# A four-layer convolution, attention and expert kernel: room, order of the last projection, depth of weight prefetch, and norm steps at the borders of its layers

## The chip, the cores and the metric

The kernel runs on one core of a Trainium2 chip. TensorE (PE) does the matrix products, VectorE (DVE) and ScalarE (ACT) the elementwise work, GpSimd (POOL) small things and some transfers, and SyncE (SP) issues most transfers. The metric is the device time of one execution in microseconds; the kernel before has a median of 3357.86 us over three runs (3353.48 to 3364.4). One further execution was recorded by the hardware profiler; all lines shown come from it. A code such as L506 is a line of the kernel before.

## The reference, cut to what matters

The input `x` is 8 x 384 x 32 x 32 in float32. Four layers follow, each `x = x + layer(gn(x))`, where `gn` normalizes each image over 32 groups of channels.

```python
# layer 0: convolutional attention, 8 heads of 48 channels
q, k, v = (einsum(pw_i, gelu(bn(depthwise3x3(x, dw_i)))) for i in "qkv")
out = bn(einsum(w_out, softmax(q.T @ k * scale) @ v))
# layer 1: 4 experts, the two best of each position mixed
out = sum_e coef_e * (w2_e @ relu(w1_e @ x + b1_e) + b2_e)
# layer 2: depthwise 7x7, reflecting edges
out = depthwise7x7(x, w) + b
# layer 3: channels in four chunks; chunks 0, 2 through a small MLP with gelu,
# chunks 1, 3 through depthwise k x k; three branches k = 1, 3, 5
x1, x2, x3 = branch(x, 1), branch(x, 3), branch(x, 5)
w = softmax(fusion(mean(x1 + x2 + x3)))
out = (x1 * w0 + x2 * w1 + x3 * w2) @ proj_w + proj_b
```

The batch norms `bn` of layer 0 run over all images and positions, so the projections can only begin when a whole convolution, of all eight images, is done. The group norms need one image each, but the kernel computes the coefficients of all images together.

## The kernel before, in words

**Tiling.** Channels lie in three blocks `ct` of 128 partitions, an image is 1024 positions. All products are float32; the profile counts each such product as two rows.

**Layer 0's convolutions** are products with banded weights (L373). Their results leave PSUM through ACT into one of two large buffers tagged `o` (L414). `results` then transposes each image on DVE (L342), takes its statistics (L164) and stores it to memory as `raw[v][b]` from SP (L344). The order of convolutions is such that v's last block comes last. The pool `co` that holds the `o` buffers closes before attention opens its pools, so attention's tiles lie in the room of it, and of the other tiles that closed with it.

**Attention** (`attention`, L437). `fetch` loads the inputs of one image; `activate(b, v)` applies the batch norm and gelu of input v on ACT, in three pieces; `project` (L506) makes k and q in 18 products each (36 rows); `spread` puts each of three tiles of the result into kT or qT, where the tile's pieces for other partitions are copied by ACT (k of the first image, L524) or DVE (L526, L528). The scale vector `own`, a mask, is made on POOL (L464 to L473). `project_v` (L553) makes v and DVE copies it into vT (L557), which POOL has set to one beforehand (L475). `scores` (L600) and the exponential on ACT (L607), then `attend` (L619) and `project_out` (L675) run over eight images, two halves, the pairs of heads and groups of positions. The very last half image has its own code at L750 to L767: `attend`, then nine products with `w_last`, then the norm of the last tile on DVE (L635 to L640), then three products which need that norm; the result z is copied by ACT (L765) and stored by POOL (L766). Three pools of PSUM tiles of two banks each, tag `sc`, rotate under k, q, v, scores and the outputs.

**Layer 1** runs the experts over images (L875, L1088). SP loads its first weights `w1` (L783), and its tiles, during attention.

**Layer 2** convolves with 7x7 banded weights (L1429): for each `ct`, eight steps `c`, each of two halves `e` of 56 rows. `load_weights` (L1152) issues the next weight tile on ACT's queue (L1159) into one of two `lw` buffers, and POOL adds the reflected edge (L1163); `next_weights` (L1168) spreads a landed tile into a `wx` buffer on ACT (L1176), and calls `load_weights` when it has spread the last part of a tile. `evict` (L1370) takes PSUM out by ACT into `o`. `finish` (L1276) then, image by image: DVE transposes `o` into `y`, adds bias and the residual `r2` (loaded by SP, two buffers), SP stores `y` to `y2mem`, DVE takes statistics, POOL copies edges (L1301). `finish_all(ct)` is stepped while the next block's convolution runs. `prepare` loads layer 2's own third input.

**Layer 3.** Its norm is done in steps: `gn_steps` (L171) first averages the means over the groups (PE, L191; DVE, L202 to L205), yields, then averages the variances (PE), takes the inverse root (DVE L158, POOL L159) and makes s and t (L209). `norm01` covers the first two channel blocks, `norm3` all. `prepare3(unit, q)` loads an input into an `xn2` buffer (two of them), applies s and t on ACT (L224) and transposes into the padded convolution input on DVE (L1348). Unit 1 holds the middle chunk (pairs of half images, `pair_s`, `pair_t`, L1457), unit 0 the first block. `convolve3(1, 5)` and `convolve3(1, 3)` (L1396) run with unit 1, step by step, while `finish_all(2)` ends; after the norm, `hidden3` (L1582 to L1607) makes the MLP's hidden values, with inputs loaded by POOL (L1587) and a bias from t (L1500). After it come unit 0's convolutions, a reordering on POOL, the fusion weights (L1740 to L1761) and the last projections (L1807 to L1818).

**What sets the order.** On PE, ACT and DVE the instructions stay in the order in which the code writes them (`manual_schedule`, L259); in layer 0's convolutions and in layers 2 and 3 this holds for POOL too. Elsewhere, for SP everywhere and for POOL in attention, a planner orders them by the program and by the room they need. Each engine takes its instructions in that order: one that waits holds all behind it. Transfers also use a small set of completion semaphores in turn, so a transfer may be held until an earlier, unrelated transfer with the same semaphore has ended.

## Time and profile before

| | us |
|---|---|
| median of three runs | 3357.86 (3353.48 to 3364.4) |
| the profiled execution's own time | 3360.26 |
| its span | 3358.5 |
| PE busy | 3150.9 (94%) |
| DVE, ACT, POOL busy | 1599.0, 1340.9, 238.1 |

The stages of that execution, in us, with PE's and ACT's busy time in each:

| stage | from - to | length | PE | ACT |
|---|---|---|---|---|
| entry and layer 0's norm | 0 - 50.6 | 50.6 | 12.18 | 16.95 |
| layer 0's convolutions | 50.6 - 287 | 236.4 | 205.57 | 179.42 |
| border to attention | 287 - 372 | 85.0 | 73.24 | 35.15 |
| attention | 372 - 1730 | 1358.0 | 1347.57 | 623.69 |
| attention's end | 1730 - 1756 | 26.0 | 18.09 | 3.52 |
| layer 1 | 1756 - 2848 | 1092.0 | 1061.87 | 248.52 |
| layer 2 | 2848 - 3017 | 169.0 | 154.64 | 95.17 |
| layer 3, to hidden3 | 3017 - 3102 | 85.0 | 46.10 | 58.04 |
| hidden3 and unit 0 | 3102 - 3232 | 130.0 | 110.82 | 69.62 |
| last projections | 3232 - 3358.5 | 126.5 | 120.83 | 10.77 |

In a line of the timeline, the first two numbers are start and duration; then engine, line, operation, output and inputs with their sizes, the number of instructions drawn together, and in brackets how long the engine was idle before and which instruction's end released it. A share of busy time is an average over stages; what an edit is worth is read from the stage that it stands in.

### The profile page before, as it was taken

The numbers are of one execution on the slowest core, as the hardware profiler recorded it, in microseconds if no ns is written. First come the engines' busy times: TensorE is split into PE (matmuls) and PEld (weight loads), VectorE is DVE, ScalarE is ACT, GpSimd is POOL, SyncE is SP. The second block draws the span as 40 slices with busy tenths as digits, with TensorE's granted clock in tenths as the row PEclk, the third lists the DMA queues.
The fourth block names the chain that finished last, engine by engine and source line by source line (L and its number), as shares of the span: only waits on it lengthen the run. The fifth ranks groups of instructions, "written<-read, shape, count | busy, mean of one in ns | idle before, by whom it ended". The sixth has DMA issues, their size and how long they took to land.

```text
span 3358.5 us, 40148 instructions
## 1 busy us (share of the span) xinstructions
PE 3150.9 (94%) x16790; PEld 1473.7 (44%) x16790; DVE 1599.0 (48%) x2189; ACT 1340.9 (40%) x1385; POOL 238.1 (7%) x395
## 2 busy tenths in 40 slices
PE   5897999999999999999989999999999998986989
PEld 4774333343434343433333444444444444655534
DVE  6996344444444444444452554343343332356064
ACT  4875453535354444445334302221121111556520
POOL 3331000000000000000000000000000000121400
PEclk9998999999999999999999999999999998997989
DMA  5886011020101110110017223121121111666666
GB/s 213 287 280 248 32 40 59 24 75 22 69 31 59 40 59 22 57 43 29 22 51 269 92 54 91 49 81 49 47 80 42 44 39 42 241 211 231 219 201 203
DMA packets 97911, 339.65 MB, mean 101 GB/s; under 512 B 14409, under 2 KB 17057, under 8 KB 93369
## 3 DMA queue, kind: packets, MB, share of 16 engines
q1 hardware_dynamic: 73816, 267.73, 23.6%
q10 hardware_dynamic: 13776, 36.90, 3.5%
q0 software_dynamic: 10128, 32.36, 2.9%
q8 instruction: 134, 2.20, 0.3%
q14 instruction: 57, 0.46, 0.0%
HBM read 237.96 MB, written 102.32 MB: 101 GB/s over the span
## 4 chain that ended last, share of the span: by engine, by line
PE 67%; issue 12%; DVE 9%; DMA 7%; ACT 4%; POOL 1%; SPq 0%; ACTq 0%; another core or an unknown queue 0%; POOLq 0%; DVEq 0%
PE av L619 13%; PE sc L600 12%; PE ph L875 9%; PE y L1088 9%; PE sc L506 7%; PE sc L553 4%; PE sc L675 3%; PE ps L1429 2%; DVE stats L164 2%; DVE y L342 2%; DMA w<-in_w 1%; PE po L1810 1%; PE po L1807 1%; PE po L1818 1%; DVE xt L309 1%
## 5 line engine op out<-in xcount | busy, mean ns | idle before, releaser
L607 ACT ACTIVATE e<-sc 128x1024 f32<-128x1024 f32 x512 | 483.1, 1030 | 545.8 <-PE sc L600 545.5
L1088 PE MATMUL y<-hs,w 128*128 128x512 f32 x1152 | 521.5, 594 | 6.2 <-DVE hs L1073 6.2
L875 PE MATMUL ph<-xn,w 128*128 128x512 f32 x1152 | 525.0, 594 | 1.3 <-ACT xn L224 1.3
L600 PE MATMUL sc<-qT,kT 64*128 64x512 f32 x2048 | 477.6, 603 | 10.4 <-ACT e L607 10.4
L619 PE MATMUL av<-e,vT 128*64 128x512 f32 x2048 | 467.5, 598 | 0.0
L879 ACT ACTIVATE hs<-ph,b 128x512 f32<-128x512 f32 x192 | 131.6, 685 | 638.5 <-PE ph L875 632.5
L1088 PEld LDWEIGHTS y<-hs,w 128*128 128x128 f32 x1152 | 217.1, 190 | 282.5 <-issue 258.4
L875 PEld LDWEIGHTS ph<-xn,w 128*128 128x128 f32 x1152 | 216.3, 190 | 268.3 <-issue 259.2
L600 PEld LDWEIGHTS sc<-qT,kT 64*128 64x128 f32 x2048 | 185.6, 186 | 297.5 <-issue 228.7
L1073 DVE TENSOR_TENSOR hs<-hs,cb 128x512 f32<-128x512 f32 x192 | 130.0, 687 | 376.6 <-ACT hs L879 370.6
L619 PEld LDWEIGHTS av<-e,vT 128*64 128x64 f32 x2048 | 135.6, 136 | 316.3 <-issue 316.3
L506 PE MATMUL sc<-y,pw 128*128 128x512 f32 x576 | 254.9, 604 | 14.1 <-ACT kT L524 9.1
L373 PE MATMUL ps<-xt,wx 64*64 64x256 f32 x3456 | 202.1, 392 | 43.1 <-ACT o L414 21.8
L637 DVE RECIPROCAL inv<-sm 128x512 f32<-128x512 f32 x64 | 214.6, 3353 | 2.2
L635 DVE LOAD_MASK_SELECT sm<-av x64 | 0.9, 14 | 420.3 <-PE av L619 420.3
L373 PEld LDWEIGHTS ps<-xt,wx 64*64 64x64 f32 x3456 | 161.3, 139 | 82.8 <-issue 50.6
L506 PEld LDWEIGHTS sc<-y,pw 128*128 128x128 f32 x576 | 110.6, 193 | 157.9 <-issue 139.5
L1429 PE MATMUL ps<-xt,wx 64*64 64x256 f32 x2688 | 158.2, 393 | 19.0 <-ACT wx L1176 13.6
L1078 DVE SCALAR_TENSOR_TENSOR r<-cb,b,r 128x512 f32<-128x512 f32 x192 | 134.3, 745 | 69.0 <-DMA cb<-cfmem 67.7
L414 ACT COPY o<-ps 128x2048 f32<-128x2048 f32 x36 | 135.3, 3763 | 47.0 <-PE ps L373 25.0
L1176 ACT ACTIVATE wx<-w,parity 128x448 f32<-128x448 f32 (+2 forms) x192 | 108.3, 616 | 104.4 <-PE ps L1429 32.8
L1429 PEld LDWEIGHTS ps<-xt,wx 64*64 64x64 f32 x2688 | 106.0, 138 | 70.1 <-ACT wx L1176 17.2
(307 smaller groups left out, 2895.6 us busy)
## 6 DMA issues: line engine op xcount, KB each, us to landing
raw<-y SPq DMA_DIRECT2D x72, 512.0 KB
y<-raw SPq DMA_DIRECT2D x24, 1536.0 KB
xr<-in_x SPq DMA_DIRECT2D x42, 512.0 KB
cb<-cfmem SPq DMA_DIRECT2D x64, 256.0 KB
w<-in_w ACTq DMA_DIRECT2D x36, 384.0 KB
xn<-in_x SPq DMA_DIRECT2D x24, 512.0 KB
x<-in_x SPq DMA_DIRECT2D x16, 768.0 KB
z<-z POOLq DMA_DIRECT2D x16, 768.0 KB, 4.2
```

The source lines that it names most:

```text
L373: nc.tensor.matmul(ps[64 * d : 64 * d + 64, 2 * i + e, cc], lhsT=w[r, 12 * cc + 6 * e + 3 * d + k, :], rhs=xt0s[ct][r, 16 * d + 8 * e + 2 ...
L414: nc.scalar.copy(o.rearrange("p b h (i c) -> p i c (b h)", i=4)[:, :, 2 * u : 2 * u + 2], ps.rearrange("p i c b h -> p i c (b h)"),)
L506: nc.tensor.matmul(ps[:, h, :], lhsT=w[:, ct, pair, :], rhs=y[:, ct, h * HF : (h + 1) * HF], start=ct == 0, stop=ct == NC - 1,)
L553: nc.tensor.matmul(ps[:, m, :C], lhsT=y[:, ct, (m0 + m) * P : (m0 + m + 1) * P], rhs=pw_v[:, ct, :], start=ct == 0, stop=ct == NC - 1,)
L600: nc.tensor.matmul(sc[:, s, :], lhsT=kTs[b][r, pair, m * P : (m + 1) * P], rhs=qTs[b][r, pair, h * HF : (h + 1) * HF], start=True, stop=True,)
L607: nc.scalar.activation(e, sc, AF.Exp, scale=1.0 if shifted else HD**-0.5)
L619: nc.tensor.matmul(av[64 * s : 64 * s + 64, :], lhsT=vT[:, m, c0 : c0 + 64], rhs=e[:, s, :], start=m == 0, stop=m == N // P - 1,)
L637: nc.vector.reciprocal(inv, sm)
L875: nc.tensor.matmul(ph, lhsT=w1[:, e, ct, dc * P : (dc + 1) * P], rhs=xn[:, ct, :], start=ct == 0, stop=ct == NC - 1,)
L1078: nc.vector.scalar_tensor_tensor(out=out[oc], in0=cb[e], scalar=b2[:, oc, e : e + 1], in1=out[oc], op0=ALU.mult, op1=ALU.add,)
L1088: nc.tensor.matmul(py[oc], lhsT=w2[:, e, dc, oc * P : (oc + 1) * P], rhs=hs, start=k == 0, stop=k == len(TODO) - 1,)
L1429: nc.tensor.matmul(ps[64 * d : 64 * d + 64, 2 * i + e, c % 2], lhsT=w[r, d * K7 + k, :], rhs=xts[ct][r, 16 * d + 8 * e + c, :, k : k + H], ...
```

## The change

It has these parts.

1. *Layer 0's start.* Block 1 of the input x is loaded into the second `o` buffer rather than into eight small buffers of a pool of its own; the pool `cy` is opened earlier. With that, the rooms of the pools move.
2. *Attention's start.* Through the moved rooms, kT and qT no longer lie where layer 0's last `o` buffer lay. vT is taken from the pool `ay` when v is first projected, and set to one there. `activate(0, 2)`, v's gelu, stands between the last product of q and its copies, rather than after them.
3. *Attention's end.* Of the nine products with `w_last`, four (two outputs, two tiles) are written ahead of the last `attend`; the first two outputs share one PSUM tile of two banks.
4. *Layer 2's weights.* Up to four tiles are loaded ahead rather than two. Tiles go in turn to two `lw` and two `xn2` buffers; two more are issued by SP at the start.
5. *Layer 3's entry.* `fetch3` issues the eight half loads of unit 1's inputs at block 2, step 5, into four `y` buffers, and `room3` clears the padding there. The second part of `norm01` is written after the first half of step 6. `prepare` of layer 2's third input is spread over six steps instead of four.
6. *norm3 and hidden3.* The first part of `norm3` comes after one step of `convolve3(1, 3)` instead of four, with `prepare3(0, 5)` to `(0, 7)` after or between its parts; the inputs of hidden3 for images 0 and 1 are issued by POOL before its second part; five steps follow instead of two.

```diff
-        x0 = co.tile([P, B, H, 32], FP, tag="o", name="o").rearrange("p b h c -> p b (h c)")
+        x0, x1 = (
+            co.tile([P, B, H, 32], FP, tag="o", name="o").rearrange("p b h c -> p b (h c)")
+            for _ in range(2)
+        )
...
-                x = cx.tile([P, N], FP, tag="x", name="x")
                 nc.sync.dma_start(out=x0[:, b], in_=a["x"][b, :, 0])
-                nc.sync.dma_start(out=x, in_=a["x"][b, :, 1])
+                nc.sync.dma_start(out=x1[:, b], in_=a["x"][b, :, 1])
...
-            vT = aw.tile([P, N // P, HEADS * 64], FP, name="vT")
-            nc.gpsimd.memset(vT, 1.0)
...
                     ps = project(w, t, y)
+                    if between and t == NC - 1:
+                        between()
...
+                if not vTs:
+                    vTs.append(ay.tile([P, N // P, HEADS * 64], FP, tag="vT", name="vT", bufs=1))
+                    nc.gpsimd.memset(vTs[0], 1.0)
...
-                    project_q(b)
-                    if begun:
-                        activate(b, 2)
+                    project_q(b, (lambda: activate(0, 2)) if begun else None)
...
+            outs = two_banks()
+            outs = [outs[:, 0, :], outs[:, 1, :]]
+            project_tiles((NC, 0), range(2))
             av_last = attend(*last, keep=True)
...
+            outs.append(two_banks()[:, 0, :])
+            project_tiles((NC, 0), (2,))
+            project_tiles((1,), range(NC))
...
-        w = lw.tile([P, 4 * K7, W + len(EDGE)], FP, tag="w", name="w")
+        n_loaded.append(c)
+        if k == K7 and more_w and (len(n_loaded) - 2) % 4 > 1:
+            w = more_w[0]()
+        else:
+            w = lw.tile([P, 4 * K7, W + len(EDGE)], FP, tag="w", name="w")
...
-            load_weights()
+            n_placed.append(key)
+
+            if len(n_loaded) - len(n_placed) < (4 if todo_load and todo_load[0][0] == K7 and more_w else 2):
+                load_weights()
...
+    more_w.append(new_xn2)
+    for _ in range(2):
+        load_weights(nc.sync)
...
+    def fetch3(q):
+
+        y = new_y()
+        for half in range(2):
+            nc.sync.dma_start(
+                out=y[64 * half : 64 * half + 64, :], in_=y2mem[HB * half + q][1, 0:64, :]
+            )
+        return y
...
+    def hidden_input(b):
+        ys = [new_y() for _ in range(2)]
+        for j in range(2):
+            nc.gpsimd.dma_start(out=ys[j], in_=y2mem[b][1 + j])
+        return ys
...
                     next_weights()
+                    if (ct, c, e) == (2, 6, 0):
+                        s01, t01 = next(norm01)
...
-                if ct == 1 and c >= 1 and c < 5:
-                    for b in (2 * c - 2, 2 * c - 1):
+                if ct == 1 and c >= 1 and c < 7:
+                    for b in ((0,), (1,), (2,), (3, 4), (5, 6), (7,))[c - 1]:
                         prepare(b)
...
                 if ct == 2 and c == 5:
+                    ys3 = [fetch3(q) for q in range(HB)]
+                    room3(1)
...
-                        prepare3(1, q)
+                        prepare3(1, q, ys3[q])
...
-        for q in range(5, B):
-            next(steps)
-            prepare3(0, q)
         next(steps)
         norm3 = gn_steps((mv3[:, 0], mv3[:, 1]), banks, order="B")
         next(norm3)
+        prepare3(0, 5)
         next(steps)
+        prepare3(0, 6)
         next(steps)
+        hidden_in = {b: hidden_input(b) for b in range(2)}
         s, t = next(norm3)
...
-        next(steps)
-        next(steps)
+        prepare3(0, 7)
+        for _ in range(5):
+            next(steps)
...
-                ys = []
-                for j in range(2):
-                    ys.append(new_y())
-                    nc.gpsimd.dma_start(out=ys[j], in_=y2mem[b][1 + j])
+                ys = hidden_in.pop(b, None) or hidden_input(b)
```

## The prediction

> **What bounds the kernel now.** I read the busy shares first, then the chain that ended last, the waits, and the timeline of each stage that the diff touches.
>
> ```profile
> PE 3150.9 (94%) x16790; PEld 1473.7 (44%) x16790; DVE 1599.0 (48%) x2189; ACT 1340.9 (40%) x1385; POOL 238.1 (7%) x395
> ...
> PE 67%; issue 12%; DVE 9%; DMA 7%; ACT 4%; POOL 1%; SPq 0%; ACTq 0%; another core or an unknown queue 0%; POOLq 0%; DVEq 0%
> ```
>
> TensorE is the bound nearly everywhere, so an edit is worth the TensorE idle time that it removes, no more. The diff removes no matmul. Its room is the holes at three borders.
>
> Layer 0 to attention, timeline of 284 to 358 us (start, duration, operation, idle before and its releaser):
>
> ```profile
> 311.50 1.02 ACT L224 ACTIVATE kT<-sc 128x1024 f32<-128x1024 f32 x1 [18.65 <-DVE y L342]
> ...
> 287.12 18.41 PE L506 MATMUL sc<-y,pw 128*128 128x512 f32 x36 [5.04 <-ACT y L224]
> 314.62 18.32 PE L506 MATMUL sc<-y,pw 128*128 128x512 f32 x36 [9.08 <-ACT kT L524]
> ...
> 336.40 16.98 PE L553 MATMUL sc<-pw_v,y 128*128 128x384 f32 x46 [0.22 <-ACT y L224]
> ...
> 313.99 0.76 SPq L490 DMA_DIRECT2D y<-raw  x1
> ...
> 315.84 0.35 SPq L239 DMA_DIRECT2D w<-in_w  x1
> ```
>
> ACT may not write kT until DVE has transposed layer 0's last outputs, whose room kT takes; so q's projection starts 9.08 us late. The v input is loaded at 313.99, ahead of the experts' weights (the w load of 2304 KB).
>
> Attention's end, then layers 2 and 3:
>
> ```profile
> 1730.39 7.09 PE L619 MATMUL av<-e,vT 128*64 128x512 f32 x32
> 1737.40 10.57 PE L675 MATMUL sc<-att,w_last 128*128 128x512 f32 x24
> ...
> 2985.19 11.10 PE L1429 MATMUL ps<-xt,wx 64*64 64x256 f32 x168 [4.75 <-ACT wx L1176]
> ...
> 3009.62 1.06 PE L191 MATMUL ps<-gn_d,gmatB 128*128 128x8 f32 x8 [1.80 <-ACT o L1370]
> ...
> 3029.52 8.74 PE L1396 MATMUL ps<-x,wx 64*64 64x128 f32 x240 [12.54 <-DVE x L1348]
> ...
> 3086.23 5.40 PE L1396 MATMUL ps<-x,wx 64*64 64x128 f32 x96 [6.83 <-DVE gn_m L202]
> ...
> 3098.44 0.62 PE L1500 MATMUL ps<-t,mw 128*72 128x8 f32 x4 [2.32 <-DVE t L1495]
> 3101.65 8.80 PE L1595 MATMUL ps<-y,mw1s 128*72 128x512 f32 x16 [2.59 <-DMA y<-y]
> ```
>
> TensorE is dense at attention's end. Layer 3 holds 12.54 + 6.83 + 2.32 + 2.59 = 24.28 us of idle.
>
> **What the Trainium skill says.** "DMA: Bandwidth & Descriptors", section "Queues, rings and completion order": each DMA engine consumes a queue's descriptors in the order of its ring. So a large SP transfer issued first delays the next one; no line of this trace shows such a pair alone. Its section "Anatomy of one DMA" gives about 2.0 us beside the data's time; in the trace hidden3's first input (512 KB), issued at 3097.70, frees TensorE at 3101.65, 3.95 later, of which the data take some 1.2, so a little more than stated. "TensorE: Matmul & The Clock Gate", section "What's actually happening": after about 3.4 us idle the array runs at half clock until about 3.4 us of work have passed. The trace agrees: 36 projection rows take 18.3 to 18.4 us after idles of 5.04 and 9.08, and 36 x 10.57 / 24 = 15.9 at the dense rate.
>
> **The parts.**
>
> *Start of layer 0* (x1 in the second `o` buffer): 0. The weights still wait for the small bn_gb load, and DVE's eight transposes (36.24 to 50.32) still set TensorE's start at 50.58. The second buffer is first needed at the first eviction, 57.55, after those. Without that cover the first eviction would wait some us.
>
> *Border to attention.* kT, qT in other room removes the 18.65 of ACT. k's projection ends at 287.12 + 18.41 = 305.5. kT's ACT work of one tile (three or four pieces of 1.0) keeps pace with 12 rows x 0.44 = 5.3, so q runs 305.5 to 321.4, against 332.9. If v followed at once, scores would move by 15 to 16. It does not, by my reading. In the changed program SP's order is: pw_v and w_out early, the raw stores, then w1, then the v input. w1's room still hangs on DVE's bn_t, so it is issued at 315.84 as now, and the v input behind it at about 316.3 instead of 313.99. DMA moved 411 to 482 GB/s from 314.5 to 329.8, here 0.42 MB/us for estimate. 2.36 MB of w1 and 1.57 MB of v input take 9.4 us; with some 1.5 us of latency v lands near 327.3. ACT's three gelus (3.5) end near 331, and q's last eviction, now behind them on ACT, near 332; DVE copies it by 335, before v's third group needs that bank. Before, the gelus ended at 337.48 and v's matmuls at 353.38, so 15.9 later; now 331 + 15.9 = 346.9, plus about 1.5 for a cold restart after 8 us idle, 348.4. Gain 5.0. Ends: the v input does not wait behind w1, 16; it lands 3 us later still, 2. vT's memset on POOL (3.51) now waits for the last raw stores, issued by 311.7, and ends near 321: hidden under the v load. `own` moves ahead of bn_s on POOL and is done long before q.
>
> *Steady attention*: 0; dense TensorE covers it.
>
> *Last projection split.* The same 24 rows (10.57) in another order. Now 18 of them (7.9) lie between the last av row at 1737.4 and the six that need its norm, which DVE ends at 1742.4 (0.72 + 3.35 + 0.69 and the gaps, 5.0). After, 8 of the 24 go ahead of the last 16 av rows: av ends near 1737.4 + 8 x 0.44 = 1740.9, its norm near 1745.9, and the 10 rows that remain as cover at 1745.3, so 0.6 of wait. outs[0] and outs[1] now share a tile, so the second product of the six waits for ACT's copy of the first (0.58) and the way there and back, some 0.9. Cost +1.5; ends +0.3 and +3. The z store behind it gates layer 1, so all of it is on the path.
>
> *Layer 2's weights four ahead.* Two buffers xn2 join lw. POOL's edge add then meets landed weights: the waits `ACT wx <- POOL w` (18.1 us, longest 5.4, most of it hidden) go. But the 4.75 at 2985.19 comes from ACT's own queue: ACT idles 8.93 there until an r2 load is in, as its weight DMA is issued in turn on a completion semaphore shared with SP. That stays. From 2848 to 3010 TensorE idles about 16 us, of which 2 to 5 are fresh weights. What is saved ahead of 2940 is partly held by DVE's finish chain with its two r2 buffers. Gain 1; ends: gain 5, loss 2 (two more 532 KB loads beside load3's).
>
> *Layer 3's entry.* The eight half loads of y2 go out near 3000, into `y` buffers, so no pair waits for xn2 (before: last load 3026). The norm's second half moves ahead by one half-step (3.2). But its matmul still needs ACT's eviction; and ACT's first layer-3 weight DMA now waits, in turn, for the second fetched half (SP issues it after the y2 store that follows DVE's last 2998.6, so it lands near 3003). Queued behind it on ACT: a spread (1.2) and the eviction (3.7), ending 3008.4. So the norm matmul comes at 3008.4 against 3009.62, and TensorE waits 3.8 there instead of 1.8; the three half-steps that remain (9.6) end at 3019 against 3017. gn_s 2.91, pair copies 2.1: 3014.8. A spread waiting for TensorE is ahead of the four affines: first affine ends 3018.1, four transposes of 1.85 end 3025.5. Gain 4.0; ends: gain 9 (the fetch is early), loss 1. POOL's memset of x goes ahead of gn_s: 0.59, done in its idle.
>
> *Norm3 and hidden3's input.* The first norm3 matmul follows one step of the 3x3 convolution, not four, and needs DVE's last bn_aggr (ends 3075.46 in DVE's timeline) and an eviction (3073.8 in ACT's). These move with the entry by 4 to 5: 3070.7. TensorE waits there, but weights then lie ready for two steps (2 x 1.45). From 3070.7: norm 1.9, steps 2.9, norm 1.7 give 3077.2; gn_s 4.16 on POOL, hidden by five steps; these are slowed by ACT, which takes the affine of image 7 and an eviction (3.67) ahead of their last weights: last step ends near 3088.5, t's product 0.6. The four hidden inputs (4 x 0.55 of POOL) are issued before gn_s, behind the last y2 store, which lands near 3075. hidden3 starts at 3089.1 against 3101.65: 12.5, of which 4.0 is counted. Gain 8.5; ends 3 and 13 (weights ready at once).
>
> *After hidden3*: 0, the order is unchanged. The 48 reorder DMAs on POOL end at 3171.2, 13.6 us ahead of their next gate.
>
> **Sum**: -5.0 + 1.5 - 1 - 4.0 - 8.5 = -17.0. Profiled execution 3360.26 (span 3358.5 and 1.8 around it): 3343.3. That execution lies 2.4 above the median of 3357.86, so for a median 3341. 0.3% is 10 us, about what a measurement of this kernel can tell from no change.
>
> **Rivals.**
> R1, v's input is not late: the stores let it in, or transfers share evenly. For it: the raw stores are out by then, and pw_v and w_out no longer lie ahead. Against it: SP's order. Then the border gives 16, and the sum -28: 3330.
> R2, layer 3's waits only change places: the weight loads with two buffers (`ACT wx L1176 <- DMA w<-in_w`, 9 us in 3010 to 3110) and DVE's chain of 42 us from eviction to bn_aggr set hidden3's start. For it: the norm waits for the same eviction. Against it: 11.7 us of idle at norm3 are pure latency. Entry and norm3 give 2 together: -5 + 1.5 - 1 - 2 = -6.5, 3351.
> R3, slower: the ACT weight DMA behind the fetched half. If that half lands late, ACT stops in order, with spreads, eviction, norm and affines behind it. It turns the sum once it lands 17 us later than 3003 for the same, 27 for a loss over 10: SP would need to hang on a store or on POOL's edge copies, and POOL's y loads of twice the size land in 4.7 now (median in 3090 to 3110). 3372.
> R4, four ahead does nothing as the stalls are of issue: it is inside the small term; without it 3342.
>
> **Chances.** Forecast (3333 to 3347) 0.45, R1 or a like larger gain 0.26, R2 0.22, R3 0.07. Lowest end by R1 with layer 3's upper end is near 3325; R2 spreads to 3354. Range 3324 to 3354. Faster by over 0.3% holds the forecast, R1 and some of R2: 0.80; within 0.13; slower 0.07.
>
> **What would show it.** q's projection near 305.5 with no wait; v's first matmul near 329 waiting on ACT gelu, that on the DMA of y; scores near 348. av of attention ending near 1741, and 1.5 us more to the z store. 3 to 4 us of TensorE wait at norm01's second half on `o`; the 12.54 down to about 6; a wait of several us at norm3's first half; hidden3 with no DMA wait. Wrong if v follows q at once, or if hidden3 starts less than 6 us earlier after the entry's shift.

## The result, and the profile after

The changed kernel takes 3345.91 us (median of 6 runs, 3342.8 to 3349.04), the kernel before in the same session 3358.57 (6 runs, 3353.48 to 3364.4). The ratio is 0.9961 with a 95% interval of 0.9949 to 0.9974: 12.7 us or 0.39% faster. The forecast was 3341, its range 3324 to 3354. The profiled execution took 3342.8 (span 3341.0).

All times below are stages of one profiled execution each, cut at the same events: the last eviction of layer 0 (ACT's copy into `o` beside which k's projection begins), the first scores, attention's end (`av<-ones,ok`), the first product of layer 1 and of layer 2, the two parts of `norm01` (first `gmatB` product of each), the first product of the 5x5 convolution, the first product of `norm3`, the first of hidden3, the first of the last projections, and the end.

| stage, us | before | after | difference | forecast |
|---|---|---|---|---|
| start to layer 0's last eviction | 289.24 | 282.74 | -6.50 | 0 |
| to the first scores | 64.07 | 58.72 | -5.35 | -5.0 |
| attention, to its end | 1394.59 | 1396.61 | +2.02 | +1.5, with the next row |
| to layer 1's first product | 31.82 | 32.63 | +0.81 | |
| layer 1 | 1060.94 | 1060.59 | -0.35 | 0 |
| layer 2, to `norm01` | 159.03 | 158.85 | -0.18 | -1 |
| `norm01` to the 5x5 convolution | 29.83 | 28.03 | -1.80 | -4.0 |
| 5x5 convolution to hidden3 | 72.13 | 66.40 | -5.73 | -8.5 |
| hidden3 to the end | 256.85 | 256.43 | -0.42 | 0 |

Without the first row the differences sum to -11.0. The first row can't be put down to the change: over the profiles of this study layer 0 ended between 282.7 and 291.2 us, with before's layer 0 at 289.24 and 285.34, and with the changed one at 282.74, 288.42, 291.23, 283.78 and others between. So the two profiles, 17.5 us apart, do not contradict medians that are 12.7 apart.

Other rows rest on one profile each too, and the experiments below hold further profiles of the same code in a stage. Before's code took 64.07 and 62.43 to the first scores, 29.83 and 33.29 from `norm01` to the 5x5 convolution, 72.13 and 70.50 from there to hidden3. The changed code took 57.9 to 60.5, 27.7 to 29.1 and 65.0 to 67.1 in eight profiles each. So each of these three gains is seen, but its size is only known to 2 or 3 us.

The page of the kernel after, busy times and the chain:

```profile
PE 3144.1 (94%) x16790; PEld 1463.5 (44%) x16790; DVE 1597.4 (48%) x2189; ACT 1341.4 (40%) x1385; POOL 237.9 (7%) x395
...
PE 27%; issue 8%; DMA 6%; DVE 4%; ACT 2%; POOL 1%; SPq 0%; ACTq 0%; DVEq 0%; POOLq 0%
```

TensorE has the same 16790 products. The shares of the chain add up to 48%, against 100% before: this chain accounts for only part of the span, and the stages are read from the timeline instead.

Layer 0 to attention, timeline of 284 to 358 us of the kernel after:

```profile
322.63 3.50 ACT L224 ACTIVATE y<-y,bn_t,bn_s 128x1024 f32<-128x1024 f32 x3 [11.81 <-DMA y<-raw]
...
283.34 31.48 PE L503 MATMUL sc<-y,pw 128*128 128x512 f32 x69
323.93 17.61 PE L558 MATMUL sc<-pw_v,y 128*128 128x384 f32 x48 [9.11 <-ACT y L224]
341.46 7.14 PE L605 MATMUL sc<-qT,kT 64*128 64x512 f32 x32
...
309.42 0.33 SPq L239 DMA_DIRECT2D w<-in_w  x1
309.84 0.38 SPq L487 DMA_DIRECT2D y<-raw  x1
```

k and q are one dense piece: the wait of 9.08 for kT is gone. A wait of 9.11 stands ahead of v. The last two lines point to its cause, which an experiment below tests: v's input is issued 0.42 after the experts' weights, and lands, gelu's start shows it, 12.8 us later.

Attention's end, timeline of 1690 to 1755 us:

```profile
1722.12 3.70 PE L680 MATMUL sc<-att,w_last 128*128 128x512 f32 x8
1725.75 3.65 PE L624 MATMUL av<-e,vT 128*64 128x512 f32 x16
1729.34 4.56 PE L680 MATMUL sc<-att,w_last 128*128 128x512 f32 x10
1734.36 1.12 PE L680 MATMUL sc<-att,w_last 128*128 128x512 f32 x2 [0.46 <-DVE att L645]
1736.16 1.98 PE L680 MATMUL sc<-att,w_last 128*128 128x512 f32 x4 [0.68 <-ACT z L775]
```

Where 24 rows stood in one piece of 10.57, there are now four pieces and two waits: one for the norm, one for ACT's copy out of the tile that two outputs share. The two waits are 1.14 together, and the four pieces take 11.36.

Layer 3's entry and `norm3`, timeline of 2970 to 3110 us, TensorE first, then ACT and SP:

```profile
3001.70 1.88 PE L191 MATMUL ps<-gn_d,gmatB 128*128 128x8 f32 x8 [6.85 <-ACT o L1408]
...
3018.17 9.21 PE L1434 MATMUL ps<-x,wx 64*64 64x128 f32 x280 [3.47 <-DVE x L1380]
...
3060.56 3.16 PE L191 MATMUL ps<-mv,gmatB 128*128 128x8 f32 x14 [10.57 <-ACT xt L1408]
...
3076.42 1.57 PE L1434 MATMUL ps<-x,wx 64*64 64x128 f32 x48 [1.70 <-ACT wx L1190]
3081.39 2.08 PE L1434 MATMUL ps<-x,wx 64*64 64x128 f32 x48 [3.41 <-ACT wx L1190]
...
3084.57 9.31 PE L1634 MATMUL ps<-y,mw1s 128*72 128x512 f32 x16 [0.53 <-DVE mw1s L1628]
```

```profile
2988.44 6.61 SPq L1365 DMA_DIRECT2D y<-y  x8
...
2996.51 0.33 ACTq L1173 DMA_DIRECT2D w<-in_w  x1
2996.96 1.23 ACT L1190 ACTIVATE wx<-xn,parity 128x448 f32<-128x448 f32 x2 [8.46 <-DMA y<-y]
...
2998.10 3.55 ACT L1408 COPY o<-ps 128x2048 f32<-128x2048 f32 x1
...
3053.33 1.12 ACT L1190 ACTIVATE wx<-w,parity 128x384 f32<-128x384 f32 x2 [3.25 <-DMA w<-in_w]
...
3055.34 1.12 ACT L1190 ACTIVATE wx<-w,parity 128x384 f32<-128x384 f32 x2 [0.89 <-DMA w<-in_w]
...
3056.87 3.64 ACT L1408 COPY xt<-ps 128x2048 f32<-128x2048 f32 x1 [0.41 <-ACT wx L1190]
```

The holes of before have changed shape rather than gone. The 12.54 ahead of the 5x5 convolution is 3.47, but 6.85 stands at the second part of `norm01`: ACT idles 8.46 until a half load issued by SP has landed, and the eviction that `norm01` needs is queued behind it. The trace names the semaphore by which each transfer reports its landing: eight of them go in turn over the transfers of SP and ACT, eight others over POOL's. ACT's weight load at 2996.51 has the same one as the second of SP's half loads, which was issued at 2989.28. Ahead of `norm3` TensorE waits 10.57 for an eviction; that eviction stands on ACT behind two spreads which waited 3.25 and 0.89 for weights. After that wait of 10.57 the granted clock of TensorE is 0.50 until 3068.6. From `norm01` to hidden3 the stretch is 94.43 long with TensorE busy for 59.41, before it was 101.96 with 60.70: 41.3 of idle became 35.0.

### The profile page after: what moved, and what is told of

It reads as the page before. It is cut to its first block, busy times and chain, and to the rows that moved or that the text cites. A ratio compares the mean times of both kernels' runs of the same rounds, so it can differ in the third digit from the quotient of the medians.

```text
span 3341.0 us, 40141 instructions
## 1 busy us (share of the span) xinstructions
PE 3144.1 (94%) x16790; PEld 1463.5 (44%) x16790; DVE 1597.4 (48%) x2189; ACT 1341.4 (40%) x1385; POOL 237.9 (7%) x395
## 5 line engine op out<-in xcount | busy, mean ns | idle before, releaser
L372 PEld LDWEIGHTS ps<-xt,wx 64*64 64x64 f32 x3456 | 154.8, 137 | 84.9 <-issue 48.1
L1467 PEld LDWEIGHTS ps<-xt,wx 64*64 64x64 f32 x2688 | 105.5, 139 | 72.1 <-ACT wx L1190 15.9
L558 PE MATMUL sc<-pw_v,y 128*128 128x384 f32 x384 | 127.8, 494 | 9.1 <-ACT y L224 9.1
```

The costliest lines, as they stand in the source:

```text
L372: nc.tensor.matmul(ps[64 * d : 64 * d + 64, 2 * i + e, cc], lhsT=w[r, 12 * cc + 6 * e + 3 * d + k, :], rhs=xt0s[ct][r, 16 * d + 8 * e + 2 ...
L1467: nc.tensor.matmul(ps[64 * d : 64 * d + 64, 2 * i + e, c % 2], lhsT=w[r, d * K7 + k, :], rhs=xts[ct][r, 16 * d + 8 * e + c, :, k : k + H], ...
```

## The experiments

Each kernel was timed beside the kernel before on the same chip. The three sessions ran on three chips; the medians of before in them were 3359.34, 3360.77 and 3362.97, and ratios are against these. Stages are cut as above. Unless another base is named, a kernel is the changed one with one thing undone or moved, and its stages are compared with those of after.

### Halves of the change: parts 1 and 2 alone, parts 3 to 6 alone

The first kernel is before with layer 0's start and attention's start changed; the second is before with the rest.

```diff
 # parts 1 and 2 alone: from the changed kernel
-            outs = two_banks()
-            outs = [outs[:, 0, :], outs[:, 1, :]]
-            project_tiles((NC, 0), range(2))
...
+            outs = [two_banks()[:, 0, :] for _ in range(NC)]
...
+            for t in (NC, *range(NC - 1)):
+                for oc in range(NC):
+                    project_tile(outs[oc], att3 if t == NC else att[:, t, :], oc, t, w_last)
...
-    more_w.append(new_xn2)
-    for _ in range(2):
-        load_weights(nc.sync)
...
-                    ys3 = [fetch3(q) for q in range(HB)]
-                    room3(1)
+                    s01, t01 = next(norm01)
...
+        for q in range(5, B):
+            next(steps)
+            prepare3(0, q)
```

> Parts 1 and 2 alone on the kernel before. In the two profiles attention's first scores come 11.85 us earlier after the change, of which 6.5 lie already in layer 0 (ACT's copy of its last PSUM tile starts at 282.74 against 289.24) and 5.35 between that copy and the scores (58.7 us against 64.1). Theory: the 5.35 are the change's, and layer 0's 6.5 are a difference between executions; then copy to scores takes 58.7 +- 0.7 here, and the time is 5 to 6 us below the kernel before. Rival: layer 0's new room is faster too; then the copy starts near 282.7 in this profile and in every one with parts 1 and 2, and the time is 11 to 12 us below.

Measured: 3358.12 (14 runs), ratio 0.9999 (0.9990 to 1.0008). The stage to the first scores is 58.21, 5.9 below before, as forecast. The total shows none of it. In the profile the stretch from `norm01` to the 5x5 convolution takes 33.29 where before takes 29.83, in code that is unchanged; ACT in the timeline of 2985 to 3040 us:

```profile
3002.74 1.23 ACT L1179 ACTIVATE wx<-w,parity 128x448 f32<-128x448 f32 x2 [5.33 <-POOL w L1166]
```

It waits 5.33 for POOL's edge of fresh weights where before waits 2.71, and layer 1 is 2.4 longer. Whether these come with the moved rooms or are what differs from one execution to the next, one profile cannot say. So the border's gain is seen in its stage, and in this kernel's total it is not (-1.2, interval -3.4 to +2.7), although 5 to 6 were expected. The rival, a faster layer 0, is not seen either: layer 0 ended at 288.42.

```diff
 # parts 3 to 6 alone: from the changed kernel
-        x0, x1 = (
-            co.tile([P, B, H, 32], FP, tag="o", name="o").rearrange("p b h c -> p b (h c)")
-            for _ in range(2)
-        )
+        x0 = co.tile([P, B, H, 32], FP, tag="o", name="o").rearrange("p b h c -> p b (h c)")
...
+            vT = aw.tile([P, N // P, HEADS * 64], FP, name="vT")
+            nc.gpsimd.memset(vT, 1.0)
...
-                    project_q(b, (lambda: activate(0, 2)) if begun else None)
+                    project_q(b)
+                    if begun:
+                        activate(b, 2)
```

> Parts 3 to 6 alone on the kernel before (layer 0's start and attention's start as before). Theory: the parts add up, so from attention's scores to the end this kernel takes what the profile of the changed kernel shows: 5.7 us less than before (last projection +2.0, layer 2 -0.3, layer 3's entry -1.7, norm3 and hidden3 -5.7), and the copy that ends layer 0 starts where it did before or, if layer 0 differs by execution alone, anywhere from 282 to 290. Rival: the parts don't add up, since the earlier parts move transfers into other company; then the gain lies outside 3 to 8 us.

Measured: 3350.82 (6 runs), 0.9970 (0.9958 to 0.9982), 8.5 below before. Attention's stage is 1396.61, the same as after; `norm01` to the 5x5 convolution 27.74, on to hidden3 66.20. The stage to the first scores, in before's code, is 62.43. A gain of 3 to 8 had been expected if the parts add up; 8.5 lies just outside, with an interval of 6.0 to 14.1. Parts 1 and 2 (-1.2) and parts 3 to 6 (-8.5) give -9.7 together against -12.7 for all, which their intervals allow: these two halves do not show an effect on each other. Inside the second half parts do act on each other, as the experiment on layer 2's weights shows.

### What holds v back: the experts' weights issued later

The changed kernel, with the weights `w1` issued by ACT during attention's first scores instead of by SP ahead of v's input.

```diff
+                if not shifted and (b, j) == (0, 4):
+                    w1s.append(load(wp, "w1", nc.scalar))
...
-    w1 = load(wp, "w1")
+    w1 = w1s[0]
```

> The changed kernel with the load of w1 taken off SP's queue and issued by ACT at the fifth score group of the first image. Theory: v's input is late because 2304 KB of w1 stand ahead of it in SP's queue; without them it is issued near 309.5 and lands near 315, ACT's gelu of v starts there instead of at 322.63, TensorE's 9.11 us wait for it falls below 2 us, and the scores come 7 to 9 us earlier: 7 to 9 us off the changed kernel's time. Rival: v's input is late of itself (its own transfer behind the raw stores and k's next input); then it still lands after 319 and the gain is under 3 us.

Measured: 3340.97 (5 runs), 0.9944 (0.9931 to 0.9957). To the first scores 53.71, another 5.0 less than after (its spread over the kernels with the same border is 57.9 to 60.5). The timeline of 284 to 358 us of this kernel, TensorE and SP:

```profile
326.54 18.47 PE L558 MATMUL sc<-pw_v,y 128*128 128x384 f32 x48 [3.59 <-ACT y L224]
...
317.91 0.33 SPq L239 DMA_DIRECT2D gate_w<-in_gate_w  x1
...
318.81 0.38 SPq L487 DMA_DIRECT2D y<-raw  x1
```

v's wait falls from 9.11 to 3.59, so `w1`'s transfer ahead in SP's queue was the larger part. The gain is smaller than the 7 to 9 expected because v's input is issued no earlier (27.6 after layer 0's last eviction, 27.1 in the kernel after): the small load `gate_w` stands in `w1`'s place on SP ahead of it, and is issued 26.7 after that eviction, just as `w1` was. With `gate_w` moved as well, in the fastest kernel below, v's input is issued 22.6 after it. The Trainium skill, "DMA: Bandwidth & Descriptors", section "Queues, rings and completion order", says that each DMA engine takes a queue's descriptors in ring order; these two kernels agree with it, with 5.5 us of waiting for 2304 KB ahead, but they can't tell order in the queue from a sharing of the engines.

### What holds `norm01`: the eight half loads from POOL

The changed kernel, with `fetch3` issuing on POOL's queue.

```diff
-            nc.sync.dma_start(
+            nc.gpsimd.dma_start(
                 out=y[64 * half : 64 * half + 64, :], in_=y2mem[HB * half + q][1, 0:64, :]
```

> The changed kernel with the eight half loads of layer 3's middle chunk issued by POOL instead of SP. Theory: ACT's 8.46 us of idle at 2996.5, and with it TensorE's 6.85 us at the second part of norm01, come from ACT's first layer-3 weight load waiting in turn for one of these half loads on a shared completion semaphore; on POOL's queue they use other semaphores, so both waits fall below 2 us, the first 5x5 product starts 5 to 8 us earlier and hidden3 4 to 7. Rival: hidden3 is set by DVE's chain from the eviction to the last statistics and by the 3x3 weight loads, which do not move with the norm; then the entry starts earlier and hidden3 moves by under 2.

Measured: 3343.27 (6 runs), 0.9949 (0.9937 to 0.9961). From the first to the second part of `norm01` 5.13 instead of 11.56. TensorE in the timeline of 2980 to 3110 us:

```profile
3002.38 1.06 PE L191 MATMUL ps<-gn_d,gmatB 128*128 128x8 f32 x8 [0.41 <-ACT o L1408]
...
3017.66 8.93 PE L1434 MATMUL ps<-x,wx 64*64 64x128 f32 x240 [4.86 <-DVE x L1380]
...
3061.28 1.87 PE L191 MATMUL ps<-mv,gmatB 128*128 128x8 f32 x8 [8.69 <-ACT xt L1408]
3065.17 1.45 PE L191 MATMUL ps<-mv,gmatB 128*128 128x8 f32 x6 [2.02 <-DVE mv L1314]
```

The wait of 6.85 is 0.41, so it was SP's half loads that held ACT's weight load and, behind it, the eviction. POOL's half loads do not land sooner (12.6 us after their issue, median); what is gained is that no weight load of ACT shares a semaphore with them. From `norm01` to the 5x5 convolution 20.41 instead of 28.03: 7.6 gained. The next stage gives 0.7 of it back: `norm3` now waits for DVE too (2.02). In the medians the kernel lies only 2.6 below after, and the intervals overlap; in its profile layer 1 is 4.0 longer, within what layer 1 differs by between profiles. So the 7.6 is shown in its stage, and the total alone shows nothing of it. The next kernel, whose total is clearly lower, has it among other changes.

### The three findings together

The changed kernel with `w1`, `gate_w` and `gate_b` loaded by ACT during attention, the last projection in before's order, and each image's two half loads shared between SP and POOL.

```diff
+                    w1s.extend([load(wp, n, nc.scalar) for n in ("w1", "gate_w", "gate_b")])
...
-            outs = two_banks()
-            outs = [outs[:, 0, :], outs[:, 1, :]]
-            project_tiles((NC, 0), range(2))
             av_last = attend(*last, keep=True)
+            outs = [two_banks()[:, 0, :] for _ in range(NC)]
+            project_tiles((NC, 0, 1), range(NC))
...
-            nc.sync.dma_start(
+            (nc.sync, nc.gpsimd)[half].dma_start(
```

> The changed kernel with w1, gate_w and gate_b loaded by ACT during attention, the last projection in its old order, and the second of each pair of half loads issued by POOL (the first stays on SP). Theory: from layer 0's last copy to the scores 50 us (53.7 with w1 alone moved, as gate_w still held v's input for 3.9 us until bn_t), 1394.6 from scores to attention's end instead of 1396.6, 5 us between the parts of norm01 instead of 11.6, conv 14 us after that; 15 to 19 us off the changed kernel in all. Rival: in layer 3 what comes earlier waits again at norm3 for ACT's eviction, and only 9 to 12 us are left.

Measured: 3325.04 (4 runs, 3323.37 to 3329.36), 0.9897 (0.9883 to 0.9911): the fastest kernel of the study, 35.7 us below before and 20.9 below after (whose median is of the first session). TensorE in the timelines of 284 to 358, 1690 to 1755 and 2960 to 3110 us:

```profile
318.40 0.91 PE L558 MATMUL sc<-pw_v,y 128*128 128x384 f32 x2 [2.72 <-ACT y L224]
...
1719.15 10.57 PE L680 MATMUL sc<-att,w_last 128*128 128x512 f32 x24
...
2984.67 1.06 PE L191 MATMUL ps<-gn_d,gmatB 128*128 128x8 f32 x8 [0.40 <-ACT o L1405]
...
3042.20 1.88 PE L191 MATMUL ps<-mv,gmatB 128*128 128x8 f32 x8 [9.86 <-ACT xt L1405]
```

To the first scores 50.30 (after: 58.72), attention 1394.59 (1396.61), on to layer 1 31.92 (32.63), `norm01` to the 5x5 convolution 20.65 (28.03): 18.5 of the 20.9, where 15 to 19 had been expected.

v waits 2.72 and its 48 rows then take 16.3, where after 3.59 and 9.11 of idle they took 18.5 and 17.6. The granted clock in the profiles explains it: it is 1.00 throughout here, and 0.50 for the first 5.5 us of v's rows after 3.59 of idle, for the first 3.8 after 9.11. The Trainium skill, "TensorE: Matmul & The Clock Gate", section "What's actually happening", puts the fall of the clock after about 3.4 us of idle. These three waits agree with that, but shorter ones do not all: in the kernel before, and in parts 3 to 6 alone, the clock fell to 0.50 for some 3.4 us within v's rows after only 2.33 of idle (before's rows took 17.9), while it held after the 2.72 here and after 2.30 in the first kernel under "Two attempts". So the length of one wait below 3.4 us does not decide it. What this kernel keeps is the 9.86 at `norm3`.

### Layer 2's weights: how far ahead, and where the input is prepared

Three kernels: the changed one with two tiles ahead; with two ahead and before's places of `prepare`; with four ahead and before's places.

```diff
 # two ahead
-    more_w.append(new_xn2)
-    for _ in range(2):
-        load_weights(nc.sync)
```

```diff
 # before's places of prepare
-                if ct == 1 and c >= 1 and c < 7:
-                    for b in ((0,), (1,), (2,), (3, 4), (5, 6), (7,))[c - 1]:
+                if ct == 1 and c >= 1 and c < 5:
+                    for b in (2 * c - 2, 2 * c - 1):
```

> The changed kernel with layer 2's weights two ahead, as before. Theory: the depth is worth nothing in layer 2 (150.6 us from its first wx wait to norm01's first part, within 1), and nothing after. Rival: it matters at layer 3's entry, since the last edge additions on POOL then come late and POOL's edge copies and with them the fetched half loads behind them; then norm01's second part or the first 5x5 product comes 3 to 6 us later, and so does the end.

> The changed kernel with layer 2's weights two ahead and the loads of layer 2's third input at four steps instead of six, both as before. Theory: with two ahead, the spread of those loads shifted which transfer each weight load on ACT waits for in turn (11.94 us for an r2 load instead of 7.81) and cost 8.4 us; with the old places layer 2 takes 150.6 +- 1 again. Rival: the loss came from elsewhere in the change (the eight half loads, the buffers); then it stays near 159.

> The changed kernel with four weights ahead, but the loads of layer 2's third input at four steps, as before. Theory: the order of transfers on ACT and SP, not the depth, decides which wait ACT meets, so layer 2 moves by more than 1 us from 150.6, either way. Rival: with four ahead ACT never needs the next weight at once, the places of the other loads are then worth nothing, and it stays within 1.

Measured: two ahead 3352.22 (5 runs), 0.9977 (0.9959 to 0.9995); two ahead with the old places 3355.13, four ahead with the old places 3350.06 (one run each). The stretch of layer 2 from the wait of 2.48 for a spread near its start (present in all of them) to `norm01`:

| us | two ahead | four ahead |
|---|---|---|
| `prepare` in before's places | 157.14 (in the kernel before 150.81) | 150.25 |
| `prepare` spread over six steps | 158.94 | 150.57 (after) |

The other kernels with four ahead lie close to after in the whole of layer 2 (156.5 to 159.6, with two ahead 167.32 and 164.95). So four ahead is worth 7 to 8 us of this stage in the changed kernel, although before, with two ahead, is as fast there; where `prepare` stands is worth at most 2. That is neither what the first kernel was expected to show (two ahead costs nothing) nor the second (before's places of `prepare` bring it back). So with the other parts in place, two ahead costs what it does not cost in before. The profile shows where. ACT in the timeline of 2838 to 2960 us, in the kernel after, in that with two ahead, and in that with two ahead and the old places, the last two with TensorE's wait behind it:

```profile
2924.78 1.23 ACT L1190 ACTIVATE wx<-w,parity 128x448 f32<-128x448 f32 x2 [7.53 <-DMA r<-r]
```

```profile
2932.12 1.23 ACT L1190 ACTIVATE wx<-w,parity 128x448 f32<-128x448 f32 x2 [11.94 <-DMA r<-r]
...
2933.40 26.93 PE L1464 MATMUL ps<-xt,wx 64*64 64x256 f32 x440 [5.34 <-ACT wx L1190]
```

```profile
2933.25 1.23 ACT L1190 ACTIVATE wx<-w,parity 128x448 f32<-128x448 f32 x2 [11.71 <-DMA r<-r]
...
2934.53 25.72 PE L1464 MATMUL ps<-xt,wx 64*64 64x256 f32 x420 [7.67 <-ACT wx L1190]
```

The weight load that ACT issues there waits for a load of the residual `r2` that SP issued: in the two kernels with two ahead for that of the last image, in after and before (7.81) for that of the image before it. The semaphores in the traces show why. In each of these kernels the weight load has the semaphore of the `r2` load for which it waits. In the two kernels with two ahead SP also issues two inputs of layer 3 (`xn<-y x2`, at 2933.77 and 2935.28) right behind the last `r2`, since `xn2` is free, and these two take the two semaphores whose turn comes just ahead of the weight load's; without them its turn would have fallen on the earlier `r2` load, as it does in before and after. TensorE's waits of 5.34 and 7.67 follow from it; in after it waits 0.78 and 1.29 in that stretch. A second wait of ACT for `r2`, 5.96 and 5.30, is put down so in these two kernels alone. With four ahead ACT idles at the first place too, 7.53 in the kernel after and 8.04 with the old places (there the profile puts it down to TensorE), but two loaded tiles more lie ready while it lasts. How the whole 7 to 8 us split over these waits was not measured.

### `norm3` and hidden3's inputs, each moved alone

The changed kernel with `norm3`'s first part in before's place, hidden3's inputs still early; then with `norm3` early, hidden3's inputs in before's place.

```diff
 # norm3 late
+        for q in range(5, B):
+            next(steps)
+            prepare3(0, q)
         next(steps)
         norm3 = gn_steps((mv3[:, 0], mv3[:, 1]), banks, order="B")
         next(norm3)
-        prepare3(0, 5)
...
-        for _ in range(5):
-            next(steps)
+        next(steps)
+        next(steps)
```

```diff
 # hidden3's inputs late
-        hidden_in = {b: hidden_input(b) for b in range(2)}
+        hidden_in = {}
```

> The changed kernel with norm3's first part after four steps again and the three last inputs prepared before it, but hidden3's inputs still loaded early. Theory: the 10.57 us wait of norm3's first part is for an eviction that does not move, so the early place only takes the three steps out from under that wait; with four steps ahead of it the wait shrinks and hidden3 starts within 2 us of the changed kernel (66.4 us after the first 5x5 product). Rival, the prediction's: the early place saves the latency of DVE, POOL and t; then hidden3 comes 5 to 8 us later, 71 to 74 us after the first 5x5 product.

> The changed kernel with the early place of norm3 but hidden3's first inputs loaded only when hidden3 is reached. Theory: the early loads are worth the 2.6 to 2.8 us of TensorE's wait for y, so hidden3 starts 68.5 to 70 us after the first 5x5 product (66.4 in the changed kernel). Rival: the early place of norm3 has already put the loads under something else, since POOL is free of gn_s 8 us before hidden3; then under 1 us is lost.

Measured: `norm3` late 3350.42 (5 runs), 0.9968 (0.9955 to 0.9981), 5x5 convolution to hidden3 69.35; inputs late 3346.06 (one run), 63.46 there. Before has 72.13, after 66.40. With `norm3` late, that is 3.0 more than after; within 2 had been expected by one reading, 5 to 8 by the other, and it lies between. TensorE then waits for the norm's coefficients as before did, 8.01 here (timeline of 2990 to 3110 us):

```profile
3083.34 4.75 PE L1434 MATMUL ps<-x,wx 64*64 64x128 f32 x96 [8.01 <-DVE gn_m L202]
```

So `norm3`'s early place is worth 3.0 in the stage, where the kernels with after's code there differ by 2. With `norm3` late, early inputs take 2.8 off (72.13 to 69.35), about the 2.59 that the kernel before waited for them, but only 1.2 off the 70.50 of the other kernel with before's code there. With `norm3` early they take nothing off: the stage is shorter without them, what follows is longer (hidden3 to the last projection 121.28, after 119.12), and from the 5x5 convolution to the end it is 322.6 against 322.8 (318.2 to 324.0 over the kernels with after's code there). Without them the waits of 1.70 and 3.41 of the last steps are one of 2.30. So with `norm3` early, no gain of the early inputs is seen, and TensorE does not wait for them.

### Two attempts at the wait of `norm3`

Both start from the fastest kernel. The first puts `norm3`'s first part after three steps, where its eviction is done, and prepares images 6 and 7 after all steps. The second prepares image 6 ahead of the last four steps, and image 7 inside hidden3's first image, behind its products.

```diff
 # first
-        next(steps)
+        for _ in range(3):
+            next(steps)
         norm3 = gn_steps((mv3[:, 0], mv3[:, 1]), banks, order="B")
...
-        prepare3(0, 7)
-        for _ in range(5):
+        for _ in range(4):
             next(steps)
+        prepare3(0, 6)
+        prepare3(0, 7)
```

```diff
 # second, from the first
+        prepare3(0, 6)
         for _ in range(4):
             next(steps)
-        prepare3(0, 6)
-        prepare3(0, 7)
...
+            if i == 0:
+                prepare3(0, 7)
```

> The last kernel but two (w1 and gates late, old last projection, split half loads) with norm3's first part after three steps, its second after one more, and the inputs of images 6 and 7 prepared after the last step. Theory: two more steps run under the wait for the eviction, and image 7's affine no longer stands ahead of the last weights on ACT, so hidden3 starts 3 to 5 us earlier than there. Rival: ACT's weight loads with two buffers pace the steps; then hidden3 moves by less than 1.5, or the later preparation is paid back after hidden3.

> As the kernel with norm3 after three steps, but image 6 is prepared before the last four steps and image 7 after hidden3's first products, so that DVE and ACT make hidden3's bias and weights ahead of image 7. Theory: what was lost there was DVE's order alone (t's product came 4 us earlier, then hidden3 waited 9.61 us for DVE); now hidden3 starts 61 to 64 us after the first 5x5 product instead of 66.3, and the time is 2 to 5 us below the kernel with the old norm place (3325). Rival: ACT, in order, pays image 7 back in hidden3's gelus or before unit 0's convolution; then the end does not move by more than 1.

Measured: the first 3335.66 (6 runs), 0.9925 (0.9911 to 0.9938); 5x5 convolution to hidden3 71.15. TensorE (timeline of 2960 to 3110 us) and DVE (3050 to 3075):

```profile
3062.78 0.42 PE L1539 MATMUL ps<-t,mw 128*72 128x8 f32 x4
3072.82 9.34 PE L1631 MATMUL ps<-y,mw1s 128*72 128x512 f32 x16 [9.61 <-DVE sums L1564]
...
3068.60 3.65 DVE L1377 STREAM_TRANSPOSE xt<-xn 128x1024 f32<-128x1024 f32 x2 [9.53 <-ACT xn L224]
```

The wait at `norm3` is gone (0.28 there) and t's product comes 61.1 after the 5x5 convolution's start, in the fastest kernel 65.2. But the next thing that hidden3 needs, the scaled weights from DVE, is queued behind the two transposes of images 6 and 7, and those wait 9.53 for ACT. Hidden3 had been expected 3 to 5 earlier; the 4 gained at t's product became a loss of 4.8 at hidden3, and of 10.6 in the median, of which the profiles explain no more than about half by this stage.

The second: 3326.99 (6 runs), 0.9899 (0.9878 to 0.9921), against 0.9897 of the fastest kernel. The stage is 63.53, as expected, 2.8 shorter than there. The total, expected 2 to 5 lower, is not: hidden3 to the last projection takes 120.16 against 118.18, and the last projections 138.08 against 136.99. In hidden3's second image TensorE waits 1.94 with nothing that the profile shows as releaser, where the fastest kernel has no wait; that is about the first of these two losses. Whether the stage's gain is paid back by image 7 inside hidden3, or lies within what runs differ by, stays open.

## Why the prediction was right

The forecast of 3341 (range 3324 to 3354), with 0.8 for faster by over 0.3%, held: 3345.91, faster by 0.39% with an interval of 0.26 to 0.51%. The mechanisms it named were found in nearly every step, but some sizes are right by luck, where two errors cancel. The stages measured here are of one profile before and one after. Its steps, in the order of its sum:

**Start of layer 0, 0.** Not contradicted, as far as it can be seen: the end of layer 0 varies by 8.5 us over the profiles, and before's two lie among those of the changed code.

**Border, -5.0: measured -5.35.** The mechanism was right at each point. q follows k without a wait. v waits for gelu and gelu for the input, which SP issues behind `w1`; 9.11 of idle against about 8 forecast. From k's first product to the scores the forecast had 61.3, measured 60.8 (280.62, where k's piece begins, to 341.46). That this is so close is luck in part: the input landed 1.8 later than forecast (42.0 after k's first product, not 40.2), while from gelu's end to the scores it took 15.3 and not 17.4. The forecast had added 1.5 for a cold restart to the 15.9 of the kernel before, but there v's rows had already run some 3.4 us at a granted clock of 0.50. R1, in which v is not late, is refuted in the changed kernel, and the experiment that takes `w1` away shows that `w1` ahead on SP was the larger part of the reason, with `gate_w` as a second one that the forecast had not named. With the border changed alone the total did not show it, and that stays open.

**Last projection, +1.5: measured +2.02, and 0.6 to 0.8 behind it.** All kernels with the new order have 1396.61, all with the old 1394.59. The two waits were named rightly and sized nearly so (0.46 and 0.68 against 0.6 and 0.9). What was left out: cut in four, the 24 rows themselves took 11.36 instead of 10.57, and the statistics on DVE which gate layer 1 come later as well (TensorE's wait for them 11.78 instead of 11.16). The term was too small by about 1.2.

**Four ahead, -1: measured about 0.** Near in size, by luck: two effects cancel of which the forecast had neither. In the changed kernel two ahead costs 8.4. The forecast had said that what ACT waits for are the turns of `r2`, and that these stay; it had not seen that with the other parts in place, two inputs of layer 3 can shift the turns and make the waits longer, and that the deeper prefetch keeps this from happening. R4, four ahead does nothing, is therefore right against before and wrong inside the changed kernel.

**Layer 3's entry, -4.0: measured -1.8** (-5.3 against the other profile with before's code there, so the total of this term is not settled). The step that was off is the time at which "the second fetched half" lands. The forecast put ACT's release 3.3 us after `norm01`'s first product; it came 6.4 after it (2996.51 against 2990.14). That half was issued in time, 0.9 ahead of `norm01`'s first product, but ACT was held until 7.2 after its issue. That the six other half loads, which SP issued in these 7.2 us, slow it is likely and not shown. So the eviction and the second part of `norm01` came 2.9 later than forecast, and the wait was 6.85 where 3.8 stood. R3 was this mechanism: it did not decide the sign, since the half came 3 late and not 17, but by this pair of profiles it took more than half of the term. The kernel with the loads on POOL takes it away and gets 7.6 in the stage.

**`norm3` and hidden3's input, -8.5: measured -5.73.** From the 5x5 convolution to `norm3` the forecast had 45.2 and it took 42.4; from there to hidden3 it had 18.4 and it took 24.0. Of the 5.6 that are missing there, 3.5 lie in the norm's first part and the two steps behind it: 8.3 (3060.56 to 3068.83), where the forecast had 1.9 and 2.9. They ran at a granted clock of 0.50 after the wait of 10.57: these two steps, 96 products, took 5.2, while in the same trace 144 such products took 4.24 at 1.00. The forecast had reckoned with a cold restart for v, and named the wait at `norm3`, but put nothing for the restart behind it. A further 1.6 lie in the five last steps (12.9 instead of 11.3), in which TensorE waits 1.70 and 3.41 for weights: the forecast had named what stands ahead of them on ACT (the affine of image 7 and an eviction), but left out that this affine first waits for its own input, 3.72 in the trace. The last 0.6 is mostly a wait of 0.53 for the scaled weights. And the early inputs were counted as part of the gain: the kernel without them shows 0.

**After hidden3, 0: measured -0.42.**

R2, that layer 3's waits only change places, is right in kind (a new 6.85, a 10.57 in place of 6.83 + 2.32 + 2.59), and by these profiles wrong in sum: entry and `norm3` give 7.5, not 2.

The gain forecast was 4 us too large by the medians and 6 by the profiles. In the profiles the terms of the last projection, four ahead, the entry and `norm3` were too favourable by 1.3, 0.8, 2.2 and 2.8, and the rest came out better than forecast by 1.1. The largest errors are a landing that was put too early and a cold clock that was not reckoned with.

## What to carry to other kernels

When a wait is taken out, look in the issue order of the queue that feeds the next consumer, and at which earlier transfer has the same completion semaphore. In this kernel v's hole came from an input that stood behind others on SP, `norm01`'s from a weight load on ACT whose turn fell on one of SP's; moving a few loads to other queues was worth 15.8 us in their stages, more than the whole change. Before an instruction is moved ahead of a wait, list what is queued behind it on its own engine; a transpose or affine that is early for its own consumer can be in the way of another. Reckon with the clock behind every long wait, and look at the granted clock of the kernel before first, so as not to count it twice. A part that shows nothing against the kernel before can still carry the others: undo it in the changed kernel before calling it worthless.

## What was not expected of the hardware

- Layer 0 differs by up to 8.5 us between profiles of kernels with the same code there (282.7 to 291.2), layer 1 by 5.3 (1059.9 to 1065.2), while the 1395 us of attention repeat to 0.01 us in every profile (1394.59 or 1396.61, by its code alone). A part of 2 us in attention can be read from one profile, one of 5 us in layer 0 cannot.
- A weight load on ACT's queue was held 8.46 us by a half load on SP's, and 7.5 to 11.9 us by a residual's load, although neither touches its data: each time the two have the same one of eight completion semaphores. Two more loads on one queue change which unrelated transfer the other queue waits for.
- TensorE's granted clock fell to 0.50 after idles of 2.33 us in two kernels, and stayed at 1.00 after 2.30 and 2.72 in two others. After 3.59 of idle it stayed low for 5.5 us of work, after 9.11 for 3.8.
